# Loading a second weight matrix during the first product, and a row-wise layout for stored counts, in a two-layer graph kernel

## The chip, the cores and the metric

The kernel runs on one core of one Trainium2 chip. The metric is device time in microseconds (us). Its engines are TensorE (PE, with PEld for its weight loads), VectorE (DVE), ScalarE (ACT), GpSimd (POOL) and SyncE (SP). SP and POOL issue the DMAs of this kernel; both queues are served by the same 16 DMA engines. Lower is better.

## What is computed

Two layers on a graph of 2500 nodes, 1024 features and 80000 edges, all in float32:

```python
h = relu(layernorm(x))
x = x + segment_sum((h @ W0)[src] * edge_weight[:, None], dst)      # layer 0
h = relu(layernorm(x))
ei = edges (src, dst) plus one self edge per node                   # layer 1
h = h @ W1.T + b
deg = number of edges that leave a node, itself counted
x = x + segment_sum(deg[row]**-0.5 * deg[col]**-0.5 * h[col], row)  # row = src, col = dst
```

The edges are sorted by dst.

## The kernel before

Nodes lie in 20 tiles of 128 rows (NT), features in 8 parts of 128 (KC). `direct` has three stages.

**W0's products.** For each tile, rows of x and of x transposed are loaded two tiles ahead (`load_tile`, L161), centred and put through relu (`transposed_rows`, L169), and multiplied with W0, which lies in eight tiles `w0` to `w7` of the pool `wpool` (L185; one tile is 128 x 1024 float32, 4 KB of a partition). The products go to `support` in DRAM (L298). Beside that, DVE and PE count edges between tiles: one-hots (L451, L453), a product (L455), an addition into `counts[t]` (L463), a [128, 20, 128] float16 tile. When the counts of a tile are whole, SP stores them into the DRAM tensor `cnat` (`store_counts`, L509, L514). For four tiles (0 to 3, "dense") weighted counts are made too (L460, L467, L471).

**Gathers, dense rows and W1's products, interleaved by a plan** (L663 to L739). A step of the plan is one of two kinds. In `gathered` (L596), POOL gathers 128 rows of `support` for 128 edges into `msg` (L601); ACT and DVE weight them and split them into `hi` (L607) and `lo` (L609), and PE multiplies both with a one-hot (L613). In `multiplied` (L623), PE multiplies the weighted counts of two dense tiles with rows of `support` that POOL loads (L635, L642). Between the steps the plan deals out pieces of other work: `finish` (L557) adds a tile's sums to x (L568, L570), stores the new x (L572), normalizes it (`normed`, L138: L144 and L150 on ACT) into `hn` and transposes it into `vT` on PE (L551, L552); `second_rows` (L580) multiplies `vT` with W1 (L586), adds the bias into `hid` (L590) and stores it (L593). The remaining counts are made here as well. The buffers `xt`, `hn` (with `hid`, which has the same name) and `vT` come from the pool `work`, two of each. W1's eight parts are put into W0's place and loaded at steps 8 to 15 of the plan (L710 to L715); the load of the bias (L717) names no order.

**The last product.** `hid` is loaded again for all tiles, scaled and split (L783 to L787). For each tile r, the stored counts `cnat[r]` are read with a DMA transpose (`counts_of`, L790, L793), cast on ACT (L795), and PE multiplies them with `hi` and `lo` of all tiles (L813). The result is added to x and stored (`row`, L798).

What sets the order: the program's order gives each instruction a priority, and the compiler lays out the instructions of each engine from a model of their times, so that an instruction whose operands are there can be pulled forward on its queue. `order_behind(i, other)` puts `i` behind `other` in that layout and adds no wait on the chip. `takes` and `count` (L482, L518) keep the planner's own clock for PE, DVE and ACT and decide how many counts follow each piece of PE work. A pool with `bufs=2` gives a new tile whichever of its two places is free.

Of the kernel before, what the change touches and what calls it, by code (L numbers as in the profile page):

```python
# [9 lines left out]
F32 = mybir.dt.float32  # L10
# [9 lines left out]
P = 128  # L20
# [19 lines left out]
OPENING = 8  # L40
BESIDE = 12
TAIL = 48

ORDER = (3, 4, 5, 6, 2, 7, 8, 9, 1, 10, 11, 12, 13, 0, 14, 15, 16, 17, 18, 19)

# [2 lines left out]
def direct(  # L48
# [44 lines left out]
    keep = ctx.enter_context(tc.tile_pool(name="keep", bufs=1))  # L93
    dram = ctx.enter_context(tc.tile_pool(name="dram", bufs=1, space=bass.MemoryType.DRAM))
    support = dram.tile([N, D], F32, name="support")
    cnat = dram.tile([NT, NT, P, P], F16, name="cnat")
    x1_d = [dram.tile([P, D], F32, name=f"x1_d{t}") for t in range(NT)]
    hid_d = [dram.tile([P, D], F32, name=f"hid_d{t}") for t in range(NT)]

# [18 lines left out]
    first = ctx.enter_context(ExitStack())  # L118
    lay = first.enter_context(tc.tile_pool(name="lay", bufs=1))
    work = first.enter_context(tc.tile_pool(name="work", bufs=2))  # L120
    psum = first.enter_context(tc.tile_pool(name="psum", bufs=2, space=bass.MemoryType.PSUM))
    ohs = first.enter_context(tc.tile_pool(name="ohs", bufs=8))
    cpool = first.enter_context(tc.tile_pool(name="cpool", bufs=3))
# [2 lines left out]
    sup = sup_ctx.__enter__()  # L126
    prep_ctx = tc.tile_pool(name="prep", bufs=1)
    prep = prep_ctx.__enter__()

    def moments(xt, pool):  # L130
        stats = pool.tile([P, 2, 6], F32, name="stats")
# [5 lines left out]

    def normed(xt, sum_, pool, behind):  # L138

        hn = pool.tile([P, D], F32, name="hn")  # L140
        mean = pool.tile([P, 2], F32, name="mean")
        nc.vector.tensor_scalar(mean[:, 0:1], sum_, -1.0 / D, None, op0=ALU.mult)
        rstd = pool.tile([P, 2], F32, name="rstd")
        i = nc.scalar.activation(hn, xt, AF.Square, bias=mean[:, 0:1], accum_out=rstd[:, 1:2])  # L144
        if behind is not None:
            order_behind(i, behind)
        nc.scalar.activation(rstd[:, 0:1], rstd[:, 1:2], AF.Sqrt, scale=1.0 / D, bias=eps)
        nc.vector.reciprocal(rstd[:, 0:1], rstd[:, 0:1])
        nc.vector.tensor_mul(mean[:, 1:2], mean[:, 0:1], rstd[:, 0:1])
        nc.scalar.activation(hn, xt, AF.Relu, scale=rstd[:, 0:1], bias=mean[:, 1:2])  # L150
        return hn

    def load_rows(t, pool):
        xt = pool.tile([P, D], F32, name="xt")
        if rows(t) < P:
            nc.vector.memset(xt, 0.0)
        nc.sync.dma_start(xt[:rows(t), :], x[t * P:t * P + rows(t), :])
        return xt


    def load_tile(t):  # L161
        xt = load_rows(t, sup)
        hT = sup.tile([P, KC, P], F32, name="hT", bufs=AHEAD + 1)
        if rows(t) < P:
            nc.gpsimd.memset(hT, 0.0)
        nc.sync.dma_start(hT[:, :, :rows(t)], xT[:, t * P:t * P + rows(t)].rearrange("(k p) n -> p k n", p=P))
        return xt, hT
# [341 lines left out]
    def store_counts(late=True):  # L509
        for entry in to_store:  # L510
            entry[0] -= 1
        while to_store and (to_store[0][0] <= 0 or not late):
            t = to_store.pop(0)[1]
            i = nc.sync.dma_start(cnat[:, t].rearrange("k p d -> p k d"), counts[t])  # L514
            if late:
                order_behind(i, last_pe)

# [15 lines left out]
                count_next(queue)  # L533


    for t in range(2, NT):
        if t + 2 >= AHEAD and t + 2 < NT:
            ready[t + 2] = transposed_rows(*load_tile(t + 2))
            takes(0.3, 4.2, 1.4)
        for _ in products(t):  # L540
            (count if t >= 4 else takes)(1.75)
        takes(s=1.2)
    sup_ctx.__exit__(None, None, None)
    gpool = first.enter_context(tc.tile_pool(name="gather", bufs=2, side="right", reuse_waits="tile"))

# [11 lines left out]
    def finish(t, sums=None):  # L557


        if sums is None:  # L560
            xt = work.tile([P, D], F32, name="xt")
            nc.sync.dma_start(xt, x1_d[t])
            sum_ = work.tile([P, 1], F32, name="sum_")
            nc.vector.tensor_add(sum_, halves[t][:, 0:1], halves[t][:, 1:2])
            for _ in range(3):
                yield 0.0, 0.0, 0.0
        else:
            xt = load_rows(t, work)  # L568
            sum_ = work.tile([P, 1], F32, name="sum_")
            nc.vector.scalar_tensor_tensor(xt, sums.rearrange("p h d -> p (h d)"), 1.0, xt,  # L570
                                           op0=ALU.mult, op1=ALU.add, accum_out=sum_)
            nc.sync.dma_start(x1_d[t], xt)  # L572
            yield 0.0, 1.25, 0.0
        hn = normed(xt, sum_, work, last_pe if sums is None else None)
        yield 0.0, 0.4, 2.7
        vT = work.tile([P, KC, P], F32, name="vT")
        yield from transposed(hn, vT)
        products_left.append(second_rows(t, vT))

    def second_rows(t, vT):  # L580

        hid = work.tile([P, D], F32, name="hn")
        for h in range(2):
            mm = psum.tile([P, 4, P], F32, name="pT").rearrange("p a b -> p (a b)")
            for k in range(KC):
                on_pe(nc.tensor.matmul(mm, vT[:, k, :], w1_sb[k][:, h * H:(h + 1) * H],  # L586
                                       start=(k == 0), stop=(k == KC - 1)))
                if k % 2 and k < KC - 1:
                    yield 1.75, 0.0, 0.0
            nc.vector.tensor_add(hid[:, h * H:(h + 1) * H], mm, bias[:, h * H:(h + 1) * H])  # L590
            if h == 0:
                yield 1.75, 0.65, 0.0
        nc.sync.dma_start(hid_d[t], hid)  # L593
        yield 1.75, 0.65, 0.0
# [28 lines left out]
    def multiplied(ts):  # L623
# [5 lines left out]
        for h in range(2):  # L629
            sums = psum.tile([P, 2, H], F32, name="mm")  # L630
            cols = slice(h * H, (h + 1) * H)
            for k0 in range(0, NT, 2):
                msg = gpool.tile([P, 2, H], F32, name="msg", bufs=8)
                if rows(k0 + 1) == P:
                    last_load = nc.gpsimd.dma_start(  # L635
                        msg, support[k0 * P:(k0 + 2) * P, cols].rearrange("(k p) d -> p k d", p=P))
                else:
                    for k in (k0, k0 + 1):
                        last_load = nc.gpsimd.dma_start(msg[:rows(k), k - k0], support[k * P:k * P + rows(k), cols])
                for k in (k0, k0 + 1):  # L640
                    for i, t in enumerate(ts):
                        m = nc.tensor.matmul(sums[:, i, :], dense[t][:rows(k), k, :], msg[:rows(k), k - k0],  # L642
                                             start=(k == 0), stop=(k == NT - 1))
                        if i == 0:
                            on_pe(m)
                    if k == NT - 1:
                        xt = work.tile([P, 2, H], F32, name="xt")
                        for i, t in enumerate(ts):
                            nc.sync.dma_start(xt[:, i], x[t * P:(t + 1) * P, cols])
                        for i, t in enumerate(ts):  # L650
                            nc.vector.scalar_tensor_tensor(xt[:, i], sums[:, i], 1.0, xt[:, i], op0=ALU.mult,
                                                           op1=ALU.add, accum_out=halves[t][:, h:h + 1])
                            nc.sync.dma_start(x1_d[t][:, cols], xt[:, i])
                        takes(v=1.25)
                        if h == 1:
                            stored.extend([4, t] for t in ts)
                            pending += PIECES * len(ts)
                    yield 1.75, 0.0, 0.0
# [23 lines left out]
    waiting, stored, products_left = [], [], []  # L682
    pending = 0
    todo = left(to_count[1])
    w1_sb = []

    def blocks_of(tiles):
        nonlocal pending
        for t in tiles:
# [16 lines left out]
    for i, is_dense in enumerate(plan):  # L706
# [1 line left out]
            rate = min(pending - (3 if i + stretch[i] < len(plan) else 0), 14) / stretch[i]  # L708
        took = next(kinds[is_dense])
        if i == OPENING:  # L710
            for k in range(KC):
                w1_sb.append(wpool.tile([P, D], F32, name=f"w{k}"))
        if i >= OPENING and (i - OPENING) < KC:
            order_behind(nc.sync.dma_start(w1_sb[i - OPENING], w1t[(i - OPENING) * P:(i - OPENING + 1) * P, :]),
                         last_load)  # L715
        if i == OPENING + KC:
            nc.sync.dma_start(bias, b1.rearrange("(o d) -> o d", o=1).to_broadcast([P, D]))  # L717
        pieces = min(pieces + rate, 2.0)
        while pieces >= 1 and products_left:
            takes(*next(products_left[0]))  # L720
# [69 lines left out]
    def counts_of(r):  # L790

        cT = work.tile([P, NT, P], F16, name="cT")
        nc.sync.dma_start_transpose(out=cT.rearrange("p t s -> p (t s)"), in_=cnat[r].rearrange("t p d -> (t p) d"))  # L793
        bT = work.tile([P, NT, P], F32R, name="bT")
        nc.scalar.copy(bT, cT)  # L795
        return bT
# [362 lines left out]
```

## Time and profile before

| What | Value |
|---|---|
| median of 3 runs | 1718.38 us (1717.27 to 1720.48) |
| the profiled execution's own time | 1716.88 us |
| its span, from the first to the last instruction | 1714.9 us |
| busy time of PE | 1646.6 us (96%) |
| busy time of DVE, ACT, POOL | 1181.0, 930.3, 521.0 us |
| mean granted TensorE clock | 0.994 |
| DMA | 351.57 MB, mean 205 GB/s |
| packets | 213585, of which 115354 under 512 bytes |
| W0's products (L287) | 13.9 to 470.1 us |
| W1's products (L586) | 580.6 to 1328.4 us |
| stores of the counts (L514) | 20, 640 KB each, issued at 133.8 to 1069.1 us, 6.3 us to landing (median) |
| loads of W1 (L714) | 8, 512 KB each, issued at 472.2 to 480.5 us, 10.9 us to landing (median) |
| transposes of the counts (L793) | 20, issued at 1308.4 to 1634.4 us, 4.6 us to landing (median) |

How to read it: a busy share is an average over the three stages, which have different limits, so the stages are looked at one by one. The rows by slices cut the span into 40 equal parts; a digit is the busy share in tenths, and PEclk is the clock that TensorE was granted. The rows of waits name what ended an engine's idle time; idle time of an engine that nobody waits for costs nothing. A float32 product of 128 x 512 appears as two records of L287, L586 or L642.

### The profile page before, as it was taken

How to read it: one execution, taken by the hardware profiler on the slowest of the kernel's cores; microseconds unless marked ns; L12 is line 12 of the kernel's file. 1: busy time of each engine (PE TensorE's matmuls, PEld its weight loads, DVE VectorE, ACT ScalarE, POOL GpSimd, SP SyncE). 2: the span in 40 equal slices, each digit the busy share in tenths (PEclk: the TensorE clock that was granted, in tenths of full speed). 3: DMA queues.
4: the chain of work that ended last, by engine and by line, in shares of the span. 5: the costliest groups of instructions: out<-in, count | busy, mean ns of one | idle time of the engine just before them, and what ended most of it. 6: DMA issues, size and time to landing. Idle time of an engine off the chain costs nothing. (4 is left out here: it accounts for less than half of the span.)

```text
span 1714.9 us, 21228 instructions
## 1 busy us (share of the span) xinstructions
PE 1646.6 (96%) x6506; PEld 1023.9 (60%) x6506; DVE 1181.0 (69%) x3043; ACT 930.3 (54%) x1516; POOL 521.0 (30%) x501
## 2 busy tenths in 40 slices
PE   6999999999989999999999999999999899999997
PEld 2466555554445555655565556665565678888886
DVE  5788888888889999999999999877772510000000
ACT  3399999982136666766565566666563411111110
POOL 3000000000056776776555466666530000000000
PEclk9999999999989999999999999999999999999999
DMA  8412211123299999899888899999875754334320
GB/s 271 170 63 66 90 53 53 62 69 93 68 349 324 385 316 352 306 347 328 299 279 265 272 332 333 355 321 323 297 270 135 229 149 113 87 84 113 83 78 21
DMA packets 213585, 351.57 MB, mean 205 GB/s; under 512 B 115354, under 2 KB 134820, under 8 KB 213462
## 3 DMA queue, kind: packets, MB, share of 16 engines
q0 software_dynamic: 60592, 219.74, 36.5%
q1 hardware_dynamic: 152870, 130.39, 24.7%
q8 instruction: 54, 0.88, 0.2%
q14 instruction: 69, 0.57, 0.1%
HBM read 282.41 MB, written 54.56 MB: 196 GB/s over the span
## 5 line engine op out<-in xcount | busy, mean ns | idle before, releaser
L607 ACT ACTIVATE hi<-msg,wgt_p 128x1024 fp32r<-128x1024 f32 x378 | 428.9, 1149 | 262.2 <-PE mm L613 168.7
L601 POOL DMA_INDIRECT msg<-support,src_p x378 | 473.4, 1252 | 271.7 <-DVE oh_r L605 75.2
L609 DVE SCALAR_TENSOR_TENSOR lo<-msg,wgt_p,hi 128x1024 fp32r<-128x1024 f32 x378 | 480.6, 1280 | 36.4 <-ACT hi L607 21.4
L287 PE MATMUL mm<-w,hT 128*128 128x512 f32 x640 | 314.8, 603 | 2.4 <-ACT hT L179 2.4
L586 PE MATMUL pT<-w,vT 128*128 128x512 f32 x640 | 308.8, 592 | 0.0
L613 PE MATMUL mm<-lo,oh_r 128*128 128x512 f32 x756 | 295.1, 471 | 8.1 <-DVE lo L609 7.7
L613 PE MATMUL mm<-hi,oh_r 128*128 128x512 f32 x756 | 279.2, 450 | 0.5 <-ACT hi L607 0.5
L460 ACT ACTIVATE wl<-oh_low,wpart 128x128 bf16<-128x128 bf16 x891 | 262.1, 414 | 0.0
L813 PE MATMUL mm<-hi,bT 128*128 128x512 f32 (+1 forms) x800 | 246.8, 391 | 3.8 <-ACT bT L795 2.0
L813 PE MATMUL mm<-lo,bT 128*128 128x512 f32 (+1 forms) x800 | 247.4, 391 | 3.2 <-DVE lo L787 3.1
L801 DVE SCALAR_TENSOR_TENSOR rows<-mm,dis,rows 128x1024 f32<-128x1024 f32 x20 | 25.7, 1284 | 306.4 <-PE mm L813 305.9
L613 PEld LDWEIGHTS mm<-lo,oh_r 128*128 128x128 f32 x756 | 135.7, 189 | 116.4 <-DVE lo L609 54.9
L453 DVE TENSOR_SCALAR oh_key<-iota,key 128x200 bf16<-128x200 f16 (+12 forms) x675 | 196.4, 293 | 4.4 <-PE cb L467 4.2
L795 ACT CAST bT<-cT 128x2560 fp32r<-128x2560 f16 x20 | 46.6, 2335 | 256.4 <-PE mm L813 256.2
L613 PEld LDWEIGHTS mm<-hi,oh_r 128*128 128x128 f32 x756 | 138.9, 189 | 68.3 <-issue 34.7
L813 PEld LDWEIGHTS mm<-lo,bT 128*128 128x128 f32 (+1 forms) x800 | 149.3, 188 | 38.9 <-DVE lo L787 8.2
L813 PEld LDWEIGHTS mm<-hi,bT 128*128 128x128 f32 (+1 forms) x800 | 149.9, 188 | 36.8 <-ACT bT L795 2.4
L463 DVE TENSOR_TENSOR counts<-cb,counts 128x200 f32 (+13 forms) x296 | 139.2, 471 | 46.8 <-PE cb L455 40.1
L451 DVE TENSOR_SCALAR oh_low<-iota,low 128x128 bf16<-128x128 f16 x675 | 169.4, 255 | 2.3 <-ACT wl L460 1.7
L642 PE MATMUL mm<-msg,dense 128*128 128x512 f32 (+1 forms) x320 | 155.3, 602 | 8.8 <-DMA msg<-support 8.8
L586 PEld LDWEIGHTS pT<-w,vT 128*128 128x128 f32 x640 | 120.0, 189 | 72.5 <-issue 56.0
L287 PEld LDWEIGHTS mm<-w,hT 128*128 128x128 f32 x640 | 108.0, 193 | 62.7 <-issue 56.7
(172 smaller groups left out, 1177.0 us busy)
## 6 DMA issues: line engine op xcount, KB each, us to landing
msg<-support POOLq DMA_DIRECT2D x36, 512.0 KB, 6.9
xt<-in_x SPq DMA_DIRECT2D x34, 512.0 KB, 6.7
cnat<-counts SPq DMA_DIRECT2D x20, 640.0 KB, 6.3
hid_d<-hn SPq DMA_DIRECT2D x20, 512.0 KB, 6.3
rows<-hid_d SPq DMA_DIRECT2D x20, 512.0 KB, 3.8
rows<-x_d SPq DMA_DIRECT2D x20, 512.0 KB, 3.8
hT<-in_xT SPq DMA_DIRECT2D x19, 512.0 KB, 3.7
support<-row SPq DMA_DIRECT2D x19, 512.0 KB, 2.9
```

The costliest lines, as they stand in the source:

```text
L287: on_pe(nc.tensor.matmul(mm[:, h, :], vT[:, k, :], ws[k][:, h * H:(h + 1) * H], start=(k == 0), stop=(k == KC - 1)))
L451: nc.vector.tensor_scalar(oh_low, iota16[:, :P], low[:, k:k + 1], None, op0=ALU.is_equal)
L453: nc.vector.tensor_scalar(oh_key[:, :NT * w], iota16[:, :NT * w], key[:, k:k + 1], None, op0=ALU.is_equal)
L460: nc.scalar.activation(wl[:, i, :], oh_low, AF.Copy, scale=wpart[:, i, k:k + 1])
L463: nc.vector.tensor_tensor(to, cb[:, :NT * w].rearrange("p (t w) -> p t w", w=w), to, op=ALU.add)
L586: on_pe(nc.tensor.matmul(mm, vT[:, k, :], w1_sb[k][:, h * H:(h + 1) * H], start=(k == 0), stop=(k == KC - 1)))
L601: nc.gpsimd.indirect_dma_start(out=msg, out_offset=None, in_=support, in_offset=bass.IndirectOffsetOnAxis(ap=src_p[:, k:k + 1], axis=0))
L607: nc.scalar.activation(hi, msg, AF.Copy, scale=wgt_p[:, k:k + 1])
L609: nc.vector.scalar_tensor_tensor(lo, msg, wgt_p[:, k:k + 1], hi.bitcast(F32), op0=ALU.mult, op1=ALU.subtract)
L613: i = nc.tensor.matmul(sums[:, h, :], oh, v[:, h * H:(h + 1) * H], start=(j == 0 and v is hi), stop=(j == n - 1 and v is lo))
L642: m = nc.tensor.matmul(sums[:, i, :], dense[t][:rows(k), k, :], msg[:rows(k), k - k0], start=(k == 0), stop=(k == NT - 1))
L813: nc.tensor.matmul(mm[:, h, :], bT[:rows(k), k, :], v[:rows(k), h * H:(h + 1) * H], start=(k == ORDER[0] and v is his[k]), stop=(k == ORDE ...
```

## The change

1. Six of W1's eight parts get places of their own (pool `ahead`, 24 KB of a partition) and are loaded one by one behind W0's products of tiles 6 to 11; the bias is loaded behind tile 12. The two parts that are left go into W0's `w6` and `w7` at step 8 of the plan.
2. The buffers `xt`, `hn` with `hid`, and `vT` leave the pool `work` and take W0's places `w0` to `w5`: each name has two places, taken strictly by turns (`big`).
3. In `cnat`, the 20 x 128 counts of a partition lie together (5 KB): a store writes 5 KB per partition where it wrote 20 pieces of 256 bytes, and the transposing read of a tile takes 2560 rows of 256 bytes that lie 5 KB apart, where it took 2560 rows that follow each other.

```diff
+EARLY = 6
...
-    cnat = dram.tile([NT, NT, P, P], F16, name="cnat")
+    cnat = dram.tile([NT, P, NT, P], F16, name="cnat")
...
+    ahead = first.enter_context(tc.tile_pool(name="ahead", bufs=1))
...
+    turns = {"xt": 0, "hn": 2, "vT": 4}
+
+    def big(name):
+        i = turns[name]
+        turns[name] = i ^ 1
+        return wpool.tile([P, D], F32, name=f"w{i}")
...
     def normed(xt, sum_, pool, behind):
-        hn = pool.tile([P, D], F32, name="hn")
+        hn = big("hn")
...
-            i = nc.sync.dma_start(cnat[:, t].rearrange("k p d -> p k d"), counts[t])
+            i = nc.sync.dma_start(cnat[t], counts[t])
...
+    w1_sb = []
     for t in range(2, NT):
...
         takes(s=1.2)
+        if 6 <= t < 6 + EARLY:
+            w1_sb.append(ahead.tile([P, D], F32, name=f"w{len(w1_sb)}"))
+            order_behind(nc.sync.dma_start(w1_sb[-1], w1t[(t - 6) * P:(t - 5) * P, :]), last_pe)
+        elif t == 6 + EARLY:
+            order_behind(nc.sync.dma_start(bias, b1.rearrange("(o d) -> o d", o=1).to_broadcast([P, D])), last_pe)
...
     def finish(t, sums=None):
-            xt = work.tile([P, D], F32, name="xt")
+            xt = big("xt")
             nc.sync.dma_start(xt, x1_d[t])
...
-            xt = load_rows(t, work)
+            xt = load_rows(t, big("xt"))
...
-        vT = work.tile([P, KC, P], F32, name="vT")
+        vT = big("vT").rearrange("p (k r) -> p k r", k=KC)
...
     def second_rows(t, vT):
-        hid = work.tile([P, D], F32, name="hn")
+        hid = big("hn")
...
     def multiplied(ts):
-                        xt = work.tile([P, 2, H], F32, name="xt")
+                        xt = big("xt").rearrange("p (i d) -> p i d", i=2)
...
         if i == OPENING:
-            for k in range(KC):
+            for k in range(EARLY, KC):
                 w1_sb.append(wpool.tile([P, D], F32, name=f"w{k}"))
-        if i >= OPENING and (i - OPENING) < KC:
-            order_behind(nc.sync.dma_start(w1_sb[i - OPENING], w1t[(i - OPENING) * P:(i - OPENING + 1) * P, :]),
-                         last_load)
-        if i == OPENING + KC:
-            nc.sync.dma_start(bias, b1.rearrange("(o d) -> o d", o=1).to_broadcast([P, D]))
+                order_behind(nc.sync.dma_start(w1_sb[k], w1t[k * P:(k + 1) * P, :]), last_load)
...
-        nc.sync.dma_start_transpose(out=cT.rearrange("p t s -> p (t s)"), in_=cnat[r].rearrange("t p d -> (t p) d"))
+        nc.sync.dma_start_transpose(out=cT.rearrange("p t s -> p (t s)"), in_=cnat[:, :, r, :].rearrange("t p d -> (t p) d"))
```

## The prediction

> **What bounds the kernel now.** I read the rows by slices first, then windows of the stretch that the change empties, then PE's waits, and last SP and ACT in order of time. The page:
>
> ```profile
> PE   6999999999989999999999999999999899999997
> DVE  5788888888889999999999999877772510000000
> PEclk9999999999989999999999999999999999999999
> DMA  8412211123299999899888899999875754334320
> ```
>
> A digit is a slice of 42.9 us. DMA is nearly idle (1 to 4) under W0's products and at 8 or 9 from slice 11 to 27, the gathers. PE stands at 9 almost everywhere, so DMA time that is saved counts only where PE waits for it. The stretch behind W0's last product, in windows (stretch, its length, busy us and instructions of PE, PEld, DVE, ACT, POOL, then PEclk, DMA share, GB/s):
>
> ```profile
> 472.00:474.00 2.00, 0.90 (x3) 0.22 (x3) 1.62 (x7) 2.00 (x1) 0.59 (x1) 1.00 0.67 131
> 476.00:478.00 2.00, 0.88 (x3) 0.32 (x3) 1.83 (x9) 0.00 (x0) 0.00 (x0) 0.50 1.03 393
> 490.00:492.00 2.00, 2.00 (x8) 0.90 (x7) 1.23 (x5) 0.72 (x1) 0.38 (x1) 1.00 1.04 409
> 508.00:512.00 4.00, 1.87 (x7) 0.92 (x6) 2.24 (x4) 1.64 (x2) 3.08 (x4) 0.98 0.95 322
> 512.00:516.00 4.00, 4.00 (x11) 2.47 (x10) 1.75 (x3) 1.15 (x1) 1.97 (x3) 0.60 1.01 399
> ```
>
> W1's eight loads are issued from 472.23 on, and the queues then run at some 400 GB/s. PE has two holes here, and behind each the granted clock falls to 0.50 to 0.60 for a while. The first hole is not a DMA's: at 472 to 478 DVE is busy 1.6 to 1.8 of 2 us with the counts' one-hots, and PE's waits in 470 to 482 are for `oh_key` (3.5 us). The second is. PE's waits from 470 to 1320:
>
> ```profile
> PE mm L642 <- DMA msg<-support: 8.8, 5, 2.9
> PE mm L613 <- DVE lo L609: 7.7, 21, 0.7
> PE cb L455 <- DVE oh_key L453: 3.5, 6, 1.0
> ```
>
> So all that PE itself waits for a DMA in the gathers is 8.8 us in 5 waits; one of them is
>
> ```profile
> 510.63 1.12 PE L642 MATMUL mm<-msg,dense 128*128 128x512 f32 x2 [2.13 <-DMA msg<-support]
> ```
>
> From 1376 to 1704 PE is busy 327.0 of 328 us with L813; nothing about loads can shorten that.
>
> **The change, part by part.** Sums are made on the profiled execution's own time, 1716.88 us (span 1714.9); the median of the runs shown, 1718.38, lies 1.5 us above, and I add 1.5 at the end.
>
> *(a) Six of W1's loads leave 472 to 481.* 6 x 512 KB = 3 MB leave. In their place come the loads that until now were pulled forward into a free work buffer at 51 to 55 us (x rows for the first `finish` and the first `multiplied`, up to 1 MB): those buffers now lie on W0's w0 and w1, which are read until 470. The relief is about 2 MB, 5 us at the 409 GB/s of the windows. Ends: nothing, and all that the stretch loses: 3.5 us of waits on `oh_key`, 2.1 us at 508, and the clock (PEclk 0.93 over 440 to 480 and 0.94 over 480 to 520: 2.8 + 2.4 us), 10.8 us. The nearest row is the second hole, the one that ends on a DMA: 2.1 us and 0.40 x 4 = 1.6 us of clock behind it, 3.7 us. I take half, 1.9: the load there landed 6.7 us after its issue at 503.89, and the median of all 36 such loads is 6.9, so that W1's traffic is not clearly what made it late. POOL's first gather waits 8.8 us there until 481.42, W1's landings named last; it was first used by PE at 496, behind 18 us of PE work without a hole, so an earlier gather is by itself worth nothing.
>
> *(b) Loads under W0's products.* Six DMAs and the bias go into SP's order after tiles 6 to 12: 7 issues of 0.3 to 0.8 us. Queued behind them are the rows and transposed rows of the next tiles, loaded two tiles (some 60 us) ahead, and the store of the support rows. DMA there has a share of 0.13 to 0.29 in windows of 40 us. Cost 0; if the cover is gone, 7 x 0.5 = 3.5 us. The bias leaves 53 us, where PE's waits in 40 to 80 us are for DVE (3.0 us): 0.
>
> *(c) Stores of the counts.* Alone in the trace, the store at 352.25 fills 353 to 356 us with shares of 0.88, 1.27 and 0.72: 2.87 us of all 16 engines for 655 KB. At 409 GB/s with a share of 1.04 (windows above, rows of 4 KB) the same bytes take 1.67 us: 1.2 us less per store, 20 stores. Ten of them fall in the full stretch (482 to 1069), 12 us of DMA. Ends on the path: 0 and the waits of PE within 20 us behind such a store: 2.56 us at 647 (L642 on its load, store at 638.68) and 2.5 us in five waits on `lo` at 584 to 594 (store at 574.84), 5.1 us together. I take half, 2.5, because 1.2 of 2.87 us goes. What is late next there is DVE, busy 37 to 39 of 40 us from 520 to 680.
>
> *(d) Work buffers on w0 to w5.* Same number, but now taken strictly by turns, where a pool of two gave the one that was free. In the order of the plan's steps, three times the buffer whose turn it is holds a `hid` whose store is only just issued, while the other is free: `normed` of tiles 8, 9 and 18. A new wait: ACT's L144 for the landing of L593. For tile 18:
>
> ```profile
> 1276.01 1.13 ACT L144 ACTIVATE hn<-xt,mean 128x1024 f32<-128x1024 f32 x1
> ...
> 1277.61 1.15 ACT L607 ACTIVATE hi<-msg,wgt_p 128x1024 fp32r<-128x1024 f32 x1
> 1278.67 1.23 ACT L150 ACTIVATE hn<-xt,mean,rstd 128x1024 f32<-128x1024 f32 x1
> ```
>
> The store is issued at 1278.05 and lands 6.3 us later (median of L593): 8.3 us later than now. Likewise 809.08 + 6.3 - 806.22 = 9.2 for tile 8 and 880.62 + 6.3 - 875.69 = 11.2 for tile 9. Queued behind it on ACT are the gathers' `hi` (L607), and for those PE waits. Below: 0, if the compiled order puts these `hi` first; the products of those tiles come 10 us and more later. Above: ACT stands all that time, and PE is covered by two `hi` buffers of 2.65 us of PE work each (1269.91 to 1272.57): 3.9 + 5.9 + 3.0 = 12.8 us. I take 0: ACT waits 168.7 us for PE in L607 alone, so it has room, and its order is laid out at compile time with the wait known.
>
> *(e) Counts read back with rows 5 KB apart.* Still 2560 rows of 256 bytes each. Before L813:
>
> ```profile
> 1308.36 8.01 SPq L793 DMA_TRANSPOSE cT<-cnat  x2
> 1316.47 0.52 SPq L593 DMA_DIRECT2D hid_d<-hn  x1
> 1318.46 4.67 SPq L793 DMA_TRANSPOSE cT<-cnat  x2
> 1329.77 0.32 SPq L593 DMA_DIRECT2D hid_d<-hn  x1
> 1331.47 0.32 SPq L783 DMA_DIRECT2D rows<-hid_d  x1
> ```
>
> Four transposes hold SP for 12.7 us, and behind them SP has 6.6 us free before the last `hid` store, which waits for PE. The other sixteen have a row of L813 each, 18 us, for a landing of 4.6 us. Cost 0 up to 1.5 times today's length; at double 12.7 - 6.6 = 6.1 us, at three times 18.8 us. No row shows strided transposes, so both ends, 0 and 18.8, are kept; I take 0, since the trace's own 256-byte pieces laid 655 KB apart (the stores of (c): 2.87 us for 655 KB) are no slower than these contiguous reads (landing in 4.6 us).
>
> A rule of the Trainium skill speaks against this part: "DMA: Bandwidth & Descriptors", Latency and other measured facts, gives DMA transposes 261 GB/s with a non-contiguous middle dimension and 350 to 400 when contiguous. By it the transposes would be an estimated 1.4 times as long, which the free 6.6 us would still hide; no run here shows it yet.
>
> Sum: -1.9 - 2.5 = -4.4, so 1712.5 on the execution's scale and **1714.0** on the runs' (-0.26%).
>
> **Rivals.** *R1, no change:* the DMA time saved was hidden: POOL still issues late, PE's order is the same, and the hole at 508 stays. For: the landing of 6.7 us. Against: waits close behind stores. (a) and (c) at 0: 1718.4. *R2, slower, the turns of (d):* place ACT L144 of tiles 8, 9, 18; price 12.8 us: 1714.0 + 12.8 = 1726.8. It decides when ACT stands over 7.9 us at each of the three places (5.3 covered, 4.4 + 3.4 us over three). Against it: the order known at compile time. *R3, slower, strided transposes:* 1714.0 + 18.8 = 1732.8 at three times the length; it decides from (6.6 + 4.4 + 3.4) / 12.7 = 1.1 more, 2.1 times.
>
> **How the numbers follow.** Forecast 0.43, R1 0.27, R2 0.20, R3 0.10. About 0.2%, 3.4 us, can be told from no change: faster 0.43, same 0.27, slower 0.30. Low end: (c) at 5.1 and (a) at 7 of its 10.8: 1718.4 - 12.1, about 1707, since both ends at once are unlikely. High end: R2 and a little, 1728; R3 and the tails are left out, 2 in 10.
>
> **What would show it.** (a) DMA below 300 GB/s at 482 to 492, and the hole before L642 near 508 shorter with a clock near 1.00. (c) No 256-byte stores; L642's waits on `msg` fall from 8.8 to about 5 us. (d) No wait of `hn` L144 on a DMA. (e) The transposes' landing near 4.6 us, L813's steady part still 18.2 us a row. I am wrong if the compiler lays the gathers in another order, or if L813 starts later.

## The result and the profile after

| | median, us | runs, us | ratio to before, 95% interval |
|---|---|---|---|
| before | 1718.38 | 1717.27 to 1721.47 (5 runs) | |
| after | 1729.62 | 1728.85 to 1730.18 (5 runs) | 1.0060 (1.0047 to 1.0073) |

The change makes the kernel 11.2 us slower, outside the predicted range. The profiled execution of after took 1730.18 us, its span 1728.3 us at a mean clock of 0.992. These are its rows by slices, to be held against those of before:

```profile
PE   6999999999999899999999999999999899999997
DVE  5788888898889899998989989878772510000000
PEclk9999999999999999999999999999999999999999
DMA  8312312212389998998877889999884653324320
```

Little stands out, since a slice is 43 us long. DMA works a little more under W0's products, where the six loads now lie; packets fell from 213585 to 164945 with the same 351.57 MB. The windows behind W0's last product (PEclk is the third figure from the end, GB/s the last) and PE's waits in the gathers. L658 is L642 of before, L629 L613, L465 L455, L567 L551, and of `normed` L155 is L144 and L161 L150; L623 is L607, the `hi`s; buffers on W0's places are called `w`. First the windows of after, then one of before, then the waits of after:

```profile
472.00:474.00 2.00, 0.96 (x3) 0.29 (x3) 1.98 (x9) 1.49 (x1) 0.03 (x1) 1.00 0.84 178
482.00:492.00 10.00, 10.00 (x31) 4.62 (x30) 5.80 (x21) 2.30 (x2) 5.03 (x6) 1.00 0.92 305
490.00:492.00 2.00, 2.00 (x7) 0.92 (x6) 1.23 (x4) 0.00 (x0) 0.52 (x1) 1.00 0.98 377
508.00:512.00 4.00, 1.71 (x6) 0.83 (x5) 2.09 (x4) 1.50 (x2) 3.11 (x3) 1.00 0.97 327
```

```profile
482.00:492.00 10.00, 10.00 (x31) 4.52 (x31) 5.98 (x24) 1.87 (x2) 5.71 (x7) 1.00 1.03 411
```

```profile
PE mm L658 <- DMA msg<-support: 7.4, 5, 3.1
PE cb L465 <- DVE oh_key L463: 5.7, 7, 2.3
PE pT L567 <- ACT w L161: 2.0, 2, 1.2
```

At 482 to 492 the queues carry 305 GB/s in place of 411: SP's queue moves 0.08 MB in place of 2.19, and the loads of POOL 2.97 in place of 1.92, so that they fill half of the room. At 490 to 492 little is left of the difference (377, 409 before), and the hole ahead of the dense products at 508 is as before (2.29 us, 2.13 before). Waits for `msg` fell from 8.8 to 7.4 us. What is new is PE's waiting for `oh_key` (3.5 to 5.7 us, the longest 2.3) and for ACT's L161.

To see where the time was lost, I matched PE's instructions of both traces and took how much later each comes in after. The lag is 1.6 us ahead of before at 517 (by before's clock), 2.7 behind at 769, where 2.0 are new; then tile 8 adds 1.9 (816), tile 9 adds 4.0 (885 to 892), tile 18 adds 1.4 (1284), and two holes whose half-clock steps (stretches in which the granted clock is 0.50) differ between the two executions add most of the rest (1.8 at 1000, 1.6 at 1379). Tile 9 in after, in order of time (start, length, engine, and in brackets the idle time before it and what ended it):

```profile
891.66 1.15 ACT L155 ACTIVATE w<-w,mean 128x1024 f32<-128x1024 f32 x1 [3.40 <-DMA hid_d<-w]
...
894.15 0.16 DVE L159 RECIPROCAL rstd<-rstd 128x1 f32<-128x1 f32 x1 [2.68 <-ACT rstd L158]
...
894.84 0.53 PE L465 MATMUL cb<-oh_key,oh_low 128*128 128x440 bf16 x1 [2.28 <-DVE oh_key L463]
```

ACT stands 3.40 us in `normed` for the landing of a `hid` store that SP issued at 885.58, and takes one more `hi` before it gives `rstd`. DVE has the next step of the same `normed` (L159) in its order and stands 2.68 us for ACT; behind it on DVE lies the one-hot `oh_key` that PE's count product wants, and PE stands 2.28 us. Its clock is then at 0.50 for 3.41 us. For tile 18, the lines that answer to those of ACT in the prediction, and PE's transposes of the same tile:

```profile
1291.36 1.15 ACT L623 ACTIVATE hi<-msg,wgt_p 128x1024 fp32r<-128x1024 f32 x1 [1.51 <-PE mm L629]
1293.63 1.15 ACT L155 ACTIVATE w<-w,mean 128x1024 f32<-128x1024 f32 x1 [1.12 <-DMA hid_d<-w]
...
1295.62 1.24 ACT L161 ACTIVATE w<-w,mean,rstd 128x1024 f32<-128x1024 f32 x1 [0.42 <-DVE mean L160]
```

```profile
1296.91 0.66 PE L567 MATMUL pT<-ident,w 128*128 128x128 f32 x4 [1.23 <-ACT w L161]
```

The store was issued at 1289.15. ACT's order has two more `hi`s ahead of this `normed` than before, and four more at each of tiles 8 and 9, and at no other tile: the compiler knew of the wait, as the prediction said. The landing is later still. Here PE stands for no one-hot but for ACT itself, 1.23 us, since its transposes of the tile (L567) lie in its order behind L161; at tile 8 it stands 0.77 us for the same and 0.51 us for DVE. The DMA transposes, last, against those of the prediction:

```profile
1320.81 7.48 SPq L803 DMA_TRANSPOSE cT<-cnat  x2
...
1330.67 5.18 SPq L803 DMA_TRANSPOSE cT<-cnat  x2
```

12.66 us of SP for four transposes, 12.68 before: rows 5 KB apart are no slower to issue.

### The profile page after: what moved, and what is told of

It is laid out like the page before. It is cut to its first block, busy times and chain, and to the rows that moved or that the text cites. A ratio compares the mean times of both kernels' runs of the same rounds, so it can differ in the third digit from the quotient of the medians.

```text
span 1728.3 us, 21213 instructions
## 1 busy us (share of the span) xinstructions
PE 1653.9 (96%) x6506; PEld 1024.1 (59%) x6506; DVE 1182.0 (68%) x3043; ACT 930.6 (54%) x1516; POOL 521.3 (30%) x501
## 2 busy tenths in 40 slices
DMA packets 164945, 351.57 MB, mean 203 GB/s; under 512 B 64154, under 2 KB 83620, under 8 KB 164822
## 5 line engine op out<-in xcount | busy, mean ns | idle before, releaser
L623 ACT ACTIVATE hi<-msg,wgt_p 128x1024 fp32r<-128x1024 f32 x378 | 429.0, 1149 | 276.0 <-PE mm L629 181.4
L602 PE MATMUL pT<-w,w 128*128 128x512 f32 x640 | 309.8, 593 | 0.0
L629 PE MATMUL mm<-lo,oh_r 128*128 128x512 f32 x756 | 295.4, 471 | 10.0 <-DVE lo L625 8.9
L629 PE MATMUL mm<-hi,oh_r 128*128 128x512 f32 x756 | 279.2, 450 | 2.0 <-ACT hi L623 1.6
L823 PE MATMUL mm<-lo,bT 128*128 128x512 f32 (+1 forms) x800 | 248.0, 392 | 3.7 <-DVE lo L797 3.7
L823 PE MATMUL mm<-hi,bT 128*128 128x512 f32 (+1 forms) x800 | 247.4, 391 | 3.2 <-ACT bT L805 2.0
L629 PEld LDWEIGHTS mm<-lo,oh_r 128*128 128x128 f32 x756 | 135.0, 189 | 120.9 <-DVE lo L625 60.4
L629 PEld LDWEIGHTS mm<-hi,oh_r 128*128 128x128 f32 x756 | 138.5, 189 | 72.8 <-issue 37.6
L823 PEld LDWEIGHTS mm<-lo,bT 128*128 128x128 f32 (+1 forms) x800 | 149.9, 188 | 39.4 <-DVE lo L797 8.5
L823 PEld LDWEIGHTS mm<-hi,bT 128*128 128x128 f32 (+1 forms) x800 | 150.4, 189 | 36.0 <-ACT bT L805 2.4
L602 PEld LDWEIGHTS pT<-w,w 128*128 128x128 f32 x640 | 120.2, 189 | 72.3 <-issue 55.3
L658 PE MATMUL mm<-msg,dense 128*128 128x512 f32 (+1 forms) x320 | 155.8, 604 | 7.4 <-DMA msg<-support 7.4
L465 PE MATMUL cb<-oh_key,oh_low 128*128 128x200 bf16 (+12 forms) x675 | 137.4, 287 | 10.3 <-DVE oh_key L463 6.1
```

Of the source, the lines that this page charges most:

```text
L623: nc.scalar.activation(hi, msg, AF.Copy, scale=wgt_p[:, k:k + 1])
L629: i = nc.tensor.matmul(sums[:, h, :], oh, v[:, h * H:(h + 1) * H], start=(j == 0 and v is hi), stop=(j == n - 1 and v is lo))
L823: nc.tensor.matmul(mm[:, h, :], bT[:rows(k), k, :], v[:rows(k), h * H:(h + 1) * H], start=(k == ORDER[0] and v is his[k]), stop=(k == ORDE ...
```

## The experiments

All times are medians, on several chips; each kernel is held against runs of before on its own chip (medians there 1718.37 to 1720.21). About 1.3 parts in a thousand is the half width of most intervals. The ratios are not quotients of the two medians and differ from these by up to 1.6 parts in a thousand, so what is told in us below is no finer than that.

| kernel | us | before there | ratio (95% interval) |
|---|---|---|---|
| e1_first_freed | 1722.36 | 1719.02 | 1.0016 (1.0003 to 1.0029) |
| e2_turns_alone | 1725.43 | 1719.02 | 1.0037 (1.0026 to 1.0047) |
| e3_layout_alone | 1721.99 | 1719.02 | 1.0017 (1.0006 to 1.0028) |
| e4_old_layout | 1725.16 | 1719.02 | 1.0026 (1.0013 to 1.0039) |
| after_again | 1728.76 | 1719.71 | 1.0057 (1.0036 to 1.0078) |
| old_layout_first_freed | 1725.33 | 1719.71 | 1.0049 (1.0031 to 1.0066) |
| layout_padded | 1723.14 | 1719.71 | 1.0019 (1.0006 to 1.0032) |
| before_itself | 1720.43 | 1720.21 | 0.9999 (0.9986 to 1.0012) |
| early_loads_alone | 1720.39 | 1720.21 | 0.9992 (0.9981 to 1.0004) |
| early_loads_repeat | 1717.05 | 1718.37 | 0.9989 (0.9978 to 1.0001) |
| store_form_only | 1723.08 | 1720.21 | 1.0013 (0.9998 to 1.0028) |
| read_form_only | 1720.01 | 1720.21 | 0.9993 (0.9981 to 1.0006) |
| one_store_new | 1721.28 | 1719.64 | 1.0005 (0.9991 to 1.0018) |
| one_store_old | 1718.99 | 1719.64 | 1.0000 (0.9986 to 1.0013) |

**The turns.** e2 is before with only this, in the pool `work`:

```diff
-        hn = pool.tile([P, D], F32, name="hn")
+        hn = big("hn")              # b2, b3 by turns
-        hid = work.tile([P, D], F32, name="hn")
+        hid = big("hn")
```

> The kernel before, with one edit: hn and hid take the two places of the pool work strictly by turns. W1, the bias, xt, vT and the counts are as before. T: 1718.4 + 7.6 = about 1726 us, with three waits of L144 on hid_d near 810, 880 and 1280 us. L and W: 1718 us, since neither loads nor layout differ.

+6.4 us, and ACT waits for stores of `hid`, by the rows of waits (us in total, times, longest) of e2 and of after:

```profile
ACT b L151 <- DMA hid_d<-b: 4.7, 3, 2.3
```

```profile
ACT w L155 <- DMA hid_d<-w: 6.6, 3, 3.4
```

In after the three waits are those of tiles 8, 9 and 18. In e2 they are tiles 8 and 9 and, between them, the second dense tile to be finished (0.75 us at 853.64), a place that the prediction doesn't list; at tile 18 ACT stands 1.32 us and the profile names DVE, but the `hid` store issued at 1284.13 landed at 1288.63, 0.2 us before ACT went on. PE falls behind there by 1.4, 1.7 and 1.6 us (tiles 8, 9, 18), 4.7 us of the 6.4, whose interval is 4.5 to 8.1 us. So the turns alone make more than half of the loss. e1 is after with `hn` and `hid` in the place that was given back first:

```diff
-        hn = big("hn")
+        hn = first_free()           # free = [2, 3]; free.pop(0)
...
         yield from transposed(hn, vT)
+        done_with(hn)               # free.append(...)
...
-        hid = big("hn")
+        hid = first_free()
...
         nc.sync.dma_start(hid_d[t], hid)
+        done_with(hid)
```

e4 is after with the three lines of `cnat` as in before.

> The changed kernel, but hn and hid take whichever of w2 and w3 was given back first, instead of strict turns; nothing else differs. Theory T (turns): ACT's L144 waited for a store of hid at tiles 8, 9 and 18, and PE fell behind there by 2.2, 4.0 and 1.5 us, 7.6 us in all; without these waits 1729.6 - 7.6 = about 1722 us, no wait of that line on hid_d in the trace. Rival L (layout of the counts) and rival W (what the moved loads displace) both expect no change: about 1729 us.

> The changed kernel with the old layout of the counts: early loads, work buffers in W0's place and turns remain. T: 1728 to 1732 us. L: 1719 to 1723 us. W: 1729 us as well, so that W and T are told apart by the first two runs and not by this one.

e1 keeps the layout and the early loads and loses 3.3 us, like the layout alone; of ACT's waits for stores of `hid` one is left, 0.7 us at the second dense tile. e4 keeps the turns and the early loads and loses 6.1 (4.5 by its ratio), like the turns alone.

**The layout.** e3 is before with the three lines of `cnat` of the change:

```diff
-    cnat = dram.tile([NT, NT, P, P], F16, name="cnat")
+    cnat = dram.tile([NT, P, NT, P], F16, name="cnat")
-            i = nc.sync.dma_start(cnat[:, t].rearrange("k p d -> p k d"), counts[t])
+            i = nc.sync.dma_start(cnat[t], counts[t])
-        ... in_=cnat[r].rearrange("t p d -> (t p) d"))
+        ... in_=cnat[:, :, r, :].rearrange("t p d -> (t p) d"))
```

> The kernel before, with the counts stored and read by the new layout alone. T: within 3 us of 1718 us, on the faster side if any, since ten stores in the gathers take some 1.2 us less of the DMA engines each. L: 1724 to 1729 us, with transposes that take visibly longer than 4.6 us to land or with a later start of the last product.

+3.0 us where the prediction's step (c) had a gain. The step at 769 is there (+2.1), as in after. The view of SP at that place, before and then e3:

```profile
753.18 0.46 SPq L514 DMA_DIRECT2D cnat<-counts  x1
754.50 9.07 SPq L157 DMA_DIRECT2D xt<-in_x  x1
```

```profile
754.35 0.45 SPq L514 DMA_DIRECT2D cnat<-counts  x1
755.65 0.33 SPq L157 DMA_DIRECT2D xt<-in_x  x1
```

Behind a store of 2560 pieces the load of x takes SP 9.07 us to issue, behind one of 128 pieces 0.33. Two kernels split the layout's halves, by reading counts that belong elsewhere (long lines broken up here and below):

```diff
 store_form_only:
-            i = nc.sync.dma_start(cnat[:, t].rearrange("k p d -> p k d"), counts[t])
+            block = cnat[t].rearrange("k p d -> (k p d)")
+            i = nc.sync.dma_start(block.rearrange("(p k d) -> p k d", p=P, k=NT), counts[t])
 read_form_only:
-        ... in_=cnat[r].rearrange("t p d -> (t p) d"))
+        whole = cnat.rearrange("k t p d -> (k t p d)").rearrange("(t p k d) -> t p k d", t=NT, p=P, k=NT)
+        ... in_=whole[:, :, r, :].rearrange("t p d -> (t p) d"))
```

> The kernel before, with the store of counts in 5 KB pieces as in the change, but the transposes reading the same contiguous 655 KB as before, so that they transpose counts that belong elsewhere: the output is not the reference's. If the store's form is what costs (SP's next load is no longer held back, the gathers near 760 to 772 come late): +2 to +4 us, the x load near 754 issued in 0.3 us, PE not whole at 768 to 772. If the transposes' rows 5 KB apart are what costs: within 1.5 us of before.

> The kernel before, with the store of counts in 2560 pieces of 256 bytes as before, but the transposes reading rows 5 KB apart as in the change; again counts that belong elsewhere, so the output is not the reference's. If the transposes' rows are what costs: +2 to +4 us, and the loss lies behind 1330, ahead of the second row of L813. If the store's form is what costs: within 1.5 us of before, with the x load near 754 held about 9 us.

The read's form costs nothing that these runs can tell (0.9993; transposes land in 4.8 us, 4.6 and 4.8 in two executions of before). With the store's form the step at 769 is back (+2.3), and the median is 2.9 us up, though its own interval just holds 1. The Trainium skill, "DMA: Bandwidth & Descriptors", Specifications, asks for 512 bytes or more of a transfer for full rate. The store itself agrees: in 752 to 776 it lands in 10.2 us after 17.1. But look at what the other queue gets in the 15.2 us that begin 1.2 us ahead of the store's issue (queue: packets, MB, share of 16 engines), 752 to 767.2 of before and then 754.67 to 769.87 of store_form_only, which runs 2.6 us later here:

```profile
q0 software_dynamic: 1132, 4.11, 71.8%
q1 hardware_dynamic: 2743, 1.44, 32.9%
```

```profile
q0 software_dynamic: 918, 3.34, 60.3%
q1 hardware_dynamic: 678, 2.41, 39.8%
```

All 16 engines are busy in both. SP's queue q1 moves 2.41 MB in place of 1.44, POOL's q0 3.34 in place of 4.11; 0.77 MB at the 380 GB/s of the second window are an estimated 2.0 us. Taken over 24 us from the same point, q0 has caught up (6.94 MB, 6.73 in before). The store's own bytes are nearly all moved by the end of both windows (2618 packets of under 512 bytes in before, of which the store has 2560 in all), so what q1 moves more is what stands behind the store: the load of x, and the `hid` store, which leaves 7.7 us behind the counts' store and not 10.8. Gathers land in 9.1 us (median over 24 us) in place of 8.2; with the old form it is 8.0 to 8.7 us in six profiles, with the new one 8.9 to 9.4 in four. PE's eight us from 768 show it. The window of before, store_form_only and the next two kernels:

```profile
768.00:776.00 8.00, 8.00 (x29) 4.73 (x28) 6.99 (x18) 6.45 (x8) 4.71 (x5) 1.00 1.03 416
```

```profile
768.00:776.00 8.00, 6.82 (x23) 3.45 (x22) 6.25 (x13) 5.38 (x6) 3.20 (x4) 1.00 1.03 417
```

The next two change that one store alone (tile 13's, the fourteenth to be issued), or all but that one:

```diff
 one_store_new:
+            if t == ORDER[0]:
+                nc.sync.dma_start(cnat[:, 13].rearrange("k p d -> p k d"), counts[t])
+            into = elsewhere if t == 13 else cnat[:, t].rearrange("k p d -> p k d")
 one_store_old:
+            into = (cnat[t].rearrange("k p d -> p k d") if t == 13 else
+                    block.rearrange("(p k d) -> p k d", p=P, k=NT))
```

> The kernel before, with one store of counts of twenty, that of tile 13 near 753, in 5 KB pieces to a place of its own (its column of the transposes' source holds the first tile's counts instead, stored once more near 134, so the output is not the reference's). If this store carries the loss: +1.5 to +3 us, the x load behind it issued in 0.3 us, PE not whole at 768 to 772 and 2 us later from 769 on. If the loss is spread over the stores: within 1 us of before, whatever is seen at 769.

> All stores of counts in 5 KB pieces except that of tile 13, which goes in 2560 pieces of 256 bytes as before (transposes contiguous, counts that belong elsewhere, so the output is not the reference's). If the store near 753 carries the loss: within 1 us of before, x load held about 9 us, PE whole at 768 to 772, no step at 769. If the loss is spread: +2 to +3 us as with all in the new form.

```profile
768.00:776.00 8.00, 6.59 (x22) 3.31 (x22) 6.05 (x16) 6.53 (x8) 3.45 (x4) 1.00 1.03 412
```

```profile
768.00:776.00 8.00, 8.00 (x29) 4.61 (x27) 7.56 (x18) 5.98 (x9) 4.75 (x5) 1.00 1.03 411
```

The hole is there with this store's new form and gone with its old one: six profiles of six with it (steps of 2.0 to 2.5 us), none of eight with the old one (old_layout_first_freed aside, below, and layout_padded, whose form is a third). With all other stores in the new form the time is that of before (1.0000). The opposite, this store alone, is 1.6 us up at an interval that holds both nothing and the whole loss. So it is shown that this store's form makes the hole at 769, and that the other nineteen bring no more than some 2 us either way; that this hole is the whole of the layout's 3 us lies within the intervals and is not shown by itself. That the load issued early is what takes the gathers' share is read from the traces and was not tried by itself.

The gain that the prediction saw is small at its place: the hole ahead of L642 near 650 is 2.56 us in before and 2.02 in before_itself, and 1.85, 1.37 and 0.93 in e3, store_form_only and one_store_old; all waits of L642 for `msg` in the gathers together are 9.7, 7.5 and 8.3 us in these (8.8 and 9.2 in the two of before).

layout_padded was to bring 256-byte pieces back within the new order, in before with rows padded to 144:

```diff
+    cnat = dram.tile([NT, P, NT, P + 16], F16, name="cnat")
+            i = nc.sync.dma_start(cnat[t][:, :, :P], counts[t])
+        ... in_=cnat[:, :, r, :P].rearrange("t p d -> (t p) d"))
```

> The kernel before with the counts in the new order of dimensions, but each row of 128 padded to 144, so that a store goes in 2560 pieces of 256 bytes again while rows of a block still lie far apart for the transposes. Theory (2560 pieces hold SP's next load back, and it is the early load that crowds out the gathers): the x load near 754 takes about 9 us to issue again, PE is whole at 768 to 772, and the time is within 1.5 us of the kernel before. Rival (rows far apart cost the transposes or the store itself): 3 us slower as with the layout alone, the x load issued in 0.3 us or L813 later.

It holds the x load for 10.5 us and PE is whole at 768 to 772, but the time is 3.4 us up, against the theory. In its trace the gathers are slow all the same (9.0 us), and PE has small new waits at 764 (0.2 us) and for `lo` at 1035 to 1095 (1.2 us, 0.2 or none in two profiles of before). Why these pieces cost more than those of before, 288 bytes from one to the next instead of 655 KB, stays open.

**The early loads.** old_layout_first_freed is e1 with the three lines of `cnat` as in before:

> Of the change only the early loads and the work buffers on W0's places are left; hn and hid take the buffer that came free first, and counts are stored as before. Theory (early loads are worth nothing; turns and layout are the whole loss): within 2 us of the kernel before, no wait of ACT for a store of hid, SP's x load near 754 held about 9 us again, PE whole at 768 to 772. Rival (the early loads do gain the 1.9 us of the prediction and something else hid it): 1.5 to 4 us faster than before. Rival (the places themselves cost): 2 us or more slower.

+5.6 us, against the theory. The rule was not that of the pool of two. At the first dense tile to be finished it gave `hn` the place of a `hid` just sent off. Rows of ACT and SP of this kernel:

```profile
774.84 1.15 ACT L167 ACTIVATE w<-w,mean 128x1024 f32<-128x1024 f32 x1 [6.30 <-DMA hid_d<-w]
```

```profile
752.92 12.00 SPq L179 DMA_DIRECT2D w<-in_x  x1
```

The x load held SP for 12 us, the `hid` store behind it left at 765.01, ACT stood 6.30 us and PE 6.17. It is the mechanism of the turns once more, at another tile, and lengthened by the old store's hold on SP; e1, with the same rule and the new layout, had sent that store at 761.04 and did not wait at this tile. For early_loads_alone each buffer was therefore given, call by call, the place that it has in before:

```diff
-    turns = {"xt": 0, "hn": 2, "vT": 4}
+    turns = {"xt": list(map(int, "0110...")), "hn": list(map(int, "2233223...")), "vT": list(map(int, "45..."))}
-        i = turns[name]
-        turns[name] = i ^ 1
-        return wpool.tile([P, D], F32, name=f"w{i}")
+        return wpool.tile([P, D], F32, name=f"w{turns[name].pop(0)}")
```

> Of the change only the early loads and the places in W0's buffers: counts stored and read as before, and each work buffer in the place, call by call, that the pool of two gave it in the kernel before. No wait of ACT for a store of hid. Theory (early loads are worth nothing): within 1.5 us of before. Rival 1 (they gain the 1.9 us of the prediction): 1.5 to 3 us faster. Rival 2 (the places in W0's buffers cost something of their own, as the 1726 us of the kernel with the first-freed order would have it): 2 to 6 us slower.

> The same kernel as early_loads_alone once more, since its interval, 0.9981 to 1.0004, leaves both no change and a gain of up to 3 us open. If the early loads gain what the prediction's step (a) took, 1.9 us: a ratio near 0.9989 again and both intervals together below 1. If they are worth nothing: a ratio of 0.9995 to 1.0010, and no kernel of this study is shown to be faster than the one before.

The mean of the two ratios is 0.9990, some 1.6 us of gain; by the medians it is +0.2 and -1.3 us. Each interval reaches 1, and taken as independent their mean runs from 0.9982 to 0.9999 (0.00115 / 1.41 to each side). The hole at 508 is 2.0 and 1.9 us in these two profiles, with a half-clock step of 3.41 us behind it as in before, so where a gain would come from isn't shown. If any version here stands ahead of before it is this one, by a hair; read_form_only has a ratio nearly as low (0.9993), and nothing there was expected to gain.

**The comparison itself.**

> The kernel before, unedited, run as if it were a change: what the comparison gives for no change at all, and a second profile of it. Expected ratio 1.000, its interval with 1 in it; the profile's holes as in the first profile, while the number of 3.41 us steps at half clock may differ. If the ratio is 1.0015 or more, the +3 us read for the layout alone is no effect of the layout.

> The changed kernel once more, unedited, beside the kernel before and the two below on one chip. If turns (+6.4 us when alone) and layout (+3.0 us when alone) add up and the early loads are worth nothing: 9 to 11 us above the kernel before, ACT waiting about 6.6 us for the stores of hid at tiles 8, 9 and 18. If the two costs overlap, because each makes the same hole of PE: 6 to 7 us above.

No change gives 0.9999. After again gives +9.1 us beside +11.2. The three parts by their ratios, +3.7, +1.7 and -1.0 parts in a thousand, make +4.4, 7.6 us; the 2 to 3 us that are left lie within the intervals. An interaction may be among them: the hole of tile 9 is 2.28 and 1.95 us in two profiles of after, 1.75 in e4 and 1.23 in e2. Only the first of them has a half-clock step at it.

## Why the prediction was wrong

- **(d), the turns: the mechanism of R2, in size half of its bound, taken at 0. This is the step that failed most: +6.4 us in e2.** The wait was right, its places too but for one, and so was that the compiler's order knows of it: only at tiles 8, 9 and 18 does `normed` lie behind more `hi`s than before, four, four and two of them (in e2 the same, in e1 none). But with these `hi`s first, which was the prediction's condition for 0, ACT still stood 2.1, 3.4 and 1.1 us. "PE is covered by two `hi` buffers" counted only the `hi`s queued behind ACT. It left out two things: DVE takes the next steps of the same `normed` (L159, L160) in order, with PE's one-hots behind them (2.28 us of PE at tile 9), and PE has the transposes of the same tile in its own order (L567, 0.77 us at tile 8 and 1.23 us at tile 18). R2's threshold of 7.9 us of ACT standing was far too high: 3.4 us were enough to cost PE 2.28 us. The 168.7 us that ACT waits for PE are a sum over all the gathers and say nothing of room at these three places.
- **(c), the stores: -2.5 predicted, about +3 measured (e3).** The DMA time saved was there (q1 takes 24.7% of the span in before and 23.0% in e3, some 28 us of all 16 engines for twenty stores), but L642's waits stayed at 7.4 to 9.7 us where about 5 were expected, and at the one place that mattered the shorter store let SP's next load go 9 us earlier, into queues that were full anyway (read from the traces, as said). The prediction asked what is late next and named DVE; it didn't ask what stands behind the store on its own queue.
- **(a), the loads that leave: -1.9 predicted, -1.6 measured, in two intervals that each reach 1.** If the sizes agree it is by luck. The traffic at 482 to 492 did fall, from 411 to 305 GB/s ("below 300" was the sign), but the hole at 508, which was to give the gain, did not: 2.0 and 1.9 us, and 2.29 in after, for 2.13. That the clock behind it is 1.00 in after says little, since the half-clock step is there in both profiles of the early loads alone.
- **(b) and (e) held.** No new wait of PE under W0's products or behind 1308; L813 (now L823) starts from the same hole of 2.0 us. The Trainium skill's rule on transposes in the prediction ("DMA: Bandwidth & Descriptors", Latency and other measured facts) would have made them an estimated 1.4 times as long; 12.66 us of SP for four, against 12.68, and landings of 4.8 us in read_form_only against 4.6 and 4.8 speak against it for these rows.
- The chances put the turns at 0.20. Against them stood the arguments that ACT has room and that a compiler which knows of a wait has dealt with it; no row of before could show that.

## What to carry to other kernels

A pool that hands out whichever buffer is free is worth time that no profile of it shows: fixed turns bring back waits for stores, and such a wait has to be followed through every engine that holds a step of the same chain in order, not just the one that waits. An order that was compiled with the wait known is no cover for it: the landing can come later on the chip than the order has room for. Before a DMA is made quicker, ask what stands behind it on its queue, and whom that will crowd.

## What the runs showed of the hardware

Between W0's last products and the end of the products, the half-clock steps of PE come in 3.41 us or twice that in all 16 profiles, at or just behind holes that are mostly 2 to 3 us, or several short ones in a row, and not each time. The same hole of 2.01 us ahead of L813's second stretch, at 1375 in before and at 1378 in before_itself, which is the same kernel (windows of 12 us):

```profile
1374.00:1386.00 12.00, 9.99 (x45) 7.92 (x44) 2.57 (x2) 4.56 (x2) 0.00 (x0) 1.00 0.99 285
```

```profile
1374.00:1386.00 12.00, 9.54 (x30) 6.70 (x29) 3.76 (x3) 5.54 (x3) 0.00 (x0) 0.72 0.88 238
```

A clock of 0.72 over 12 us is 3.4 us lost in one execution and none in the other. "TensorE: Matmul & The Clock Gate" of the Trainium skill, Part 1, tells of a free-running window of some 3.4 us, which fits a fall that depends on when the hole comes; it lets the clock fall after an idle window of that length, where holes of 2 us are enough here. Such steps are one reason why single executions of one kernel differ by several us (before: 1713.98 to 1725.95 in all its runs), and why the 13 us between the two profiles were not all the change's.
